# Head products of a small attention layer in half tiles of 64 rows, and the written order of its stage made anew

## The chip, the core and the metric

The kernel runs on one core of a Trainium2 chip. The metric is the device time of one execution in microseconds; the time of a kernel is the median of its runs. A core has five engines that run side by side, each through its own instructions in order: TensorE (matrix products; PE in the profile, its weight loads PEld), VectorE (DVE), ScalarE (ACT), GpSimd (POOL) and SyncE (SP), which here issues nearly all DMAs. Engines wait for each other through semaphores. Products are written to PSUM, which the kernel uses as 8 banks of 128 partitions x 512 numbers; ScalarE and VectorE read them from there.

## The reference, cut to what matters

The program is a small vision tower: patches of 32 images become 256 tokens of 256 features each, then two layers follow, each an attention part and an FFN part. The change lies in the second FFN ("Layer-1 FFN"), which is itself an attention over four heads with four experts each:

```python
sx = jnp.einsum('bsh,ndh->bnsd', x, hl_w) + hl_b[None, :, None, :]      # heads: 4 x 64 rows
q = jnp.einsum('bnsd,neod->bneso', sx, wq)                               # four experts per head
k = jnp.einsum('bnsd,nod->bnso', sx, wk)
v = jnp.einsum('bnsd,nod->bnso', sx, wv)
scores = jnp.einsum('bnesd,bntd->bnest', q, k) * d ** 0.5 + causal
att = jax.nn.softmax(scores, axis=-1)
qkv = jnp.einsum('bnest,bntd->bnesd', att, v)
...
gs = jax.nn.softmax(jnp.einsum('bnsf,nef->bnse', out, gate_w) + gate_b[None, :, None, :], axis=-1)
mixed = jnp.einsum('bnsed,bnse->bnsd', out.reshape(b, nh, s, ne, d), gs)
hn = layernorm(mixed + resid, ln_g, ln_b)
...
hx = jax.nn.relu(jnp.where(pm, 0.0, fx @ fc1_w.T + fc1_b))
hx = jnp.where(pm, 0.0, hx @ fc2_w.T + fc2_b)
hx = layernorm(hx + fx, fnorm_g, fnorm_b)
fg = jax.nn.softmax(fout @ fgate_w.T, axis=-1)
return (fout.reshape(b, s, nh, d) * fg[..., None]).reshape(b, s, h)
```

The line with `sx` is the head product that the change cuts in two: for each image a 256 x 256 weight times the 256 x 256 features. All is 32-bit.

## The kernel before, in words

The stage of the Layer-1 FFN takes the images one by one through about 90 small steps, called pieces. `PIECES` (L1556) is their list; a piece is named by its place there. The steps of one image, in the order of the data, with the engine that does them:

- `features_in` (piece 0, a DMA issued by SP): the normed features come in as `exT`. `heads` (3, L1164, TensorE): the head products, into one bank. `heads_out` (4, ScalarE): into `sx`, with bias; SP issues two DMAs that copy it with the halves of partitions swapped (`sw`).
- `experts` 0, 1 (5, 7, TensorE) and `experts_out` (6, 8, ScalarE, two copies each): the queries `g`. `head_values` (9, TensorE) and `head_values_out` (10, 11, VectorE): `ev`.
- `scores` 0 to 4 (12 to 16, TensorE, two banks each) and `exponentials` (18 to 22, ScalarE): `et`. `outputs` 0 to 3 (31 to 34, TensorE; 0 and 2 take four banks each) and `outputs_out` 0 to 7 (39 to 46, ScalarE).
- `gate_logits`, `gate_softmax`, `mixed`, `summed`, `squares 0`, `squares_sum 0`, `root 0`, `scaled` (47 to 65): VectorE, with `squares`, `root` and one exponential on ScalarE.
- `turn_e` (66): VectorE turns blocks of 32 x 32 and SP writes them to DRAM (`er_turned`). `moved_e` (2, L1435): SP reads them back in another order (`fraw`, two DMAs), which waits until the write has landed. `turned_e` (67, ScalarE): scale and bias into `fxT`. `features_moved` (92): two DMAs of `fxT` to `both`. `features_zero` (68, VectorE) counts zeros.
- `first_layer` (69, TensorE), `first_layer_out` (70, ScalarE, and four DMAs of `hx` to `both`), `second_layer` (71, TensorE), `second_layer_out` (72, 73, VectorE).
- `squares 1` (74), `squares_sum 1` (75), `root 1` (76), `head_gate` 0 to 8 (77 to 85), `last_norm` (86 to 91: 4, 0, 1, 2, 3, and 5, which is the DMA to the output).

What sets the order of the work is written out by hand in two tables. The kernel turns off the scheduler for this stage (`manual_schedule`, L1630), and `order_e` (L1620) yields the pieces: `ROUND` (L1575) is one round, in which each entry is (back, piece), and round r does the piece for image r - back. So -8 is the earliest stage of an image and -1 the last: at one time 8 images are in the pipeline. At the head product of the last image (`LAST`) the rounds stop, and `END` (L1586) lists all that is left, as (how far from the last image, piece). Each engine runs its pieces in the order in which these tables name them. A bank is taken in turn out of 8, so the product that takes a bank waits until the one that had it eight takes ago has been read. Most buffers of the stage exist once or twice (`p1`, `p2`), `et` eight times.

Every product is issued by the helper `mm` at L118, so TensorE's work has one line in the profile, and groups are told apart by their tiles. A product's shape, such as `128*64`, is rows by columns of the array that its weights take. A 32-bit product shows as two records. `halves` is the two slices of 64 partitions.

Of the kernel before, what the change touches and what calls it, by code (L numbers as in the profile page):

```python
# [40 lines left out]
P = 128  # L41
B, N, D = 32, 256, 256
# [38 lines left out]
def vit_tower(tc, a, out):  # L81
# [17 lines left out]
    def bank():  # L99
        return ppool.tile([P, 512], F32, name="bank", tag="bank")  # L100
# [11 lines left out]
    def load(pool, name, eng=nc.scalar):  # L112
        t = pool.tile(list(a[name].shape), F32, name=f"w_{name}")
        eng.dma_start(t, a[name])
        return t

    def mm(o, lhsT, rhs, first=True, last=True):
        nc.tensor.matmul(o, lhsT, rhs, start=first, stop=last)  # L118
# [187 lines left out]
    with (  # L306
# [7 lines left out]
        for k, n in enumerate(PARTS):  # L314
            f = sum(PARTS[:k])
            x, w = pw.tile([P, n, N], F32, name=f"patch0_{k}"), pw.tile([P, n, D], F32, name=f"tokW{k}")
# [4 lines left out]
        p = bank()  # L321
# [296 lines left out]
    hl = load(pwe, "hl_t", nc.sync)  # L618
# [495 lines left out]
    with (  # L1114
# [19 lines left out]
        halves = [slice(h * HD, (h + 1) * HD) for h in range(2)]  # L1134
# [29 lines left out]
        def heads(b, im):  # L1164
            p = im.ph = bank()
            for hp in range(2):
                for k in range(2):
                    mm(p[:, hp * N : (hp + 1) * N], hl[:, k, hp * P : (hp + 1) * P], im.f[:, k], k == 0, k == 1)

        def heads_out(b, im):  # L1170
            im.sx = p2.tile([P, 2, N], F32, name="sx")
# [362 lines left out]
        def last_norm(b, im, i):  # L1534
# [20 lines left out]
        images = [Image() for _ in range(B)]  # L1555
        PIECES = (  # L1556
            (features_in,), (residual,), (moved_e,), (heads,), (heads_out,), (experts, 0), (experts_out, 0),
            (experts, 1), (experts_out, 1), (head_values,), (head_values_out, 0), (head_values_out, 1),
            (scores, 0), (scores, 1), (scores, 2), (scores, 3), (scores, 4), (nothing,), (exponentials, 0),
# [13 lines left out]
            (features_moved,), (count_bad, 0), (count_bad, 1), (count_bad, 2), (count_bad, 3),  # L1573
        )
        ROUND = (  # L1575
            (-2, 2), (-3, 54), (-1, 72), (-3, 56), (-4, 42), (-6, 4), (-1, 73), (-4, 33), (-1, 74), (-4, 34),
            (-4, 44), (-3, 57), (-4, 45), (-1, 75), (-3, 58), (-3, 59), (-6, 1), (-6, 5), (-4, 43), (-1, 76),
            (-4, 46), (-6, 6), (-5, 16), (-5, 12), (-5, 22), (-1, 77), (-6, 30), (-5, 18), (-2, 67), (-6, 9),
            (-1, 87), (-5, 13), (-4, 47), (-5, 14), (-2, 92), (-2, 69), (-6, 10), (-1, 78), (-5, 19),
            (-6, 11), (-1, 79), (-3, 60), (-4, 48), (-5, 20), (-3, 61), (-6, 7), (-5, 15), (-2, 68),  # L1580
            (-1, 80), (-2, 70), (-1, 89), (-3, 62), (-1, 81), (-4, 49), (-1, 82), (-6, 8), (-1, 88),
            (-3, 63), (-3, 64), (-1, 83), (-5, 31), (-1, 84), (-4, 50), (-5, 32), (-1, 85), (-1, 86),
            (-7, 3), (-8, 0), (-1, 90), (-3, 65), (-5, 21), (-4, 51), (-1, 91), (-5, 41), (-3, 66), (-5, 40),
            (-5, 39), (-4, 52), (-4, 53), (-4, 55), (-2, 71), (-1, 93), (-1, 94), (-1, 95), (-1, 96),
        )
        END = (  # L1586
            (0, 2), (3, 51), (4, 65), (2, 40), (3, 52), (2, 39), (2, 42), (2, 41), (2, 21), (0, 1), (3, 53),
            (4, 66), (3, 54), (3, 55), (5, 71), (3, 56), (6, 90), (3, 57), (5, 72), (4, 2), (2, 33), (2, 34),
            (0, 4), (5, 73), (5, 74), (3, 58), (2, 43), (5, 75), (2, 44), (3, 59), (1, 15), (5, 76), (2, 46),
            (2, 45), (5, 77), (2, 47), (5, 78), (6, 91), (2, 48), (0, 7), (1, 21), (4, 67), (3, 60), (0, 9),  # L1590
            (2, 49), (3, 61), (4, 92), (2, 50), (5, 79), (4, 69), (0, 10), (0, 5), (0, 8), (2, 51), (3, 62),
            (2, 52), (5, 80), (0, 11), (5, 87), (2, 53), (3, 63), (1, 13), (4, 70), (3, 64), (2, 54),
            (5, 81), (2, 55), (4, 68), (1, 14), (5, 82), (2, 56), (3, 65), (0, 6), (5, 89), (3, 66), (2, 57),
            (1, 19), (1, 16), (1, 12), (1, 20), (0, 12), (5, 83), (5, 88), (4, 71), (1, 18), (1, 22),
            (2, 58), (0, 18), (4, 72), (3, 2), (4, 73), (2, 59), (4, 74), (4, 75), (1, 31), (1, 32), (1, 33),
            (1, 41), (1, 34), (1, 42), (1, 39), (1, 40), (4, 76), (3, 67), (2, 60), (5, 84), (0, 30),
            (5, 85), (3, 69), (2, 61), (5, 86), (5, 90), (1, 44), (3, 68), (0, 13), (1, 43), (2, 62),
            (1, 45), (2, 63), (3, 92), (1, 46), (5, 91), (3, 70), (0, 14), (1, 47), (4, 77), (0, 16),
            (2, 64), (1, 48), (4, 78), (1, 49), (4, 79), (1, 50), (4, 80), (1, 51), (2, 65), (1, 52),
            (1, 53), (4, 81), (2, 66), (0, 22), (0, 15), (4, 82), (0, 19), (1, 55), (1, 54), (0, 20),  # L1600
            (4, 87), (3, 71), (4, 83), (1, 56), (0, 31), (4, 89), (1, 57), (4, 84), (3, 72), (0, 21),
            (1, 58), (0, 32), (0, 40), (3, 73), (4, 85), (1, 59), (4, 88), (1, 60), (0, 41), (0, 42),
            (3, 74), (2, 2), (3, 75), (0, 39), (2, 67), (1, 61), (0, 33), (0, 43), (4, 86), (4, 90), (0, 34),
            (0, 44), (3, 76), (3, 77), (1, 62), (1, 63), (2, 69), (2, 92), (3, 78), (4, 91), (2, 68),
            (2, 70), (1, 64), (1, 65), (3, 79), (0, 46), (0, 45), (0, 47), (3, 80), (1, 66), (0, 48),
            (3, 81), (0, 49), (3, 87), (3, 82), (1, 2), (2, 71), (0, 50), (3, 83), (0, 51), (3, 89), (0, 52),
            (3, 84), (3, 88), (0, 53), (3, 85), (0, 55), (0, 54), (2, 72), (2, 73), (0, 56), (2, 74),
            (3, 86), (0, 57), (2, 75), (3, 90), (2, 76), (0, 58), (3, 91), (1, 67), (2, 77), (0, 59),
            (2, 78), (0, 60), (2, 87), (2, 79), (1, 92), (0, 61), (2, 80), (2, 89), (1, 69), (2, 81),
            (1, 70), (0, 62), (1, 68), (2, 82), (1, 71), (2, 83), (0, 63), (0, 64), (2, 84), (2, 88),  # L1610
            (2, 85), (0, 65), (0, 66), (2, 90), (1, 73), (0, 67), (1, 72), (2, 86), (0, 69), (0, 92),
            (1, 74), (1, 75), (2, 91), (0, 70), (0, 68), (0, 71), (0, 93), (0, 72), (0, 73), (0, 74),
            (0, 94), (1, 76), (0, 75), (1, 77), (0, 76), (0, 95), (1, 78), (0, 77), (0, 87), (0, 78),
            (1, 79), (1, 87), (1, 80), (0, 79), (0, 96), (1, 81), (0, 80), (1, 82), (1, 89), (1, 83),
            (0, 81), (0, 89), (0, 82), (0, 83), (1, 84), (1, 88), (0, 84), (1, 85), (0, 88), (0, 85),
            (1, 86), (1, 90), (1, 91), (0, 90), (0, 86), (0, 91),
        )
        LAST = PIECES.index((heads,))

        def order_e():  # L1620
# [406 lines left out]
```

## Time and profile before

| | |
|---|---|
| median of 3 runs | 1806.92 us (1803.8 to 1807.66) |
| profiled execution | 1813.98 us, its span 1812.2 us |
| granted TensorE clock | 0.987 |
| TensorE, VectorE, ScalarE busy, of the span | 97%, 72%, 43% |
| first head product of the stage, fifth, last | 1241.0, 1288.2, 1733.6 us |
| all pieces of the stage that are not DMAs done | 1807.6 us |

The profile is of one execution. A row of groups gives line, engine, operation, tiles written and read, shape, count, then busy time in us, mean length of one in ns, idle time before it, and who ended that idle time. A row of waits gives the engine and its instruction, what it waited for, the time in total, how often, and the longest. In the order of time each row has its start, its length, and the group. In the chain that ended last each row has its start, its length and the work that the end hung on. "issue" is time for which the profile shows no reason.

### The profile page before, as it was taken

To read this page: it belongs to the slowest core of one execution; us is meant where nothing else is said; L and a number is where in the kernel's file an instruction comes from. 1 tells how busy PE (TensorE), PEld (TensorE's weight loads), DVE (VectorE), ACT (ScalarE), POOL (GpSimd) and SP (SyncE) were. 2 spreads that over 40 slices of the span, in tenths; PEclk is the share of its full clock that TensorE was granted. 3 is DMA by queue.
4 is the path that set the end of the run, shared out by engine and by line. 5 is a ranking of instruction groups with operands and counts; after the bars stand their busy time and mean duration, and the time that the engine had idled before them with its cause. 6 is when DMAs were issued, how large, how long until landed. Compare 5 with 4: busy or idle time off the path is not lost.

```text
span 1812.2 us, 43832 instructions
## 1 busy us (share of the span) xinstructions
PE 1763.8 (97%) x18072; PEld 1267.4 (70%) x18072; DVE 1309.8 (72%) x3580; ACT 776.5 (43%) x1607; POOL 445.5 (25%) x506
## 2 busy tenths in 40 slices
PE   9999999999999999999999999999999999999993
PEld 7888566667576676767654555557888888888882
DVE  2335367787878665444458877875699999999998
ACT  0000322222222212121244554555888888888883
POOL 1223234343434335333344433341000000000000
PEclk9999999999999999999999999999999999999995
DMA  8552112121211115233312222112244444444432
GB/s 274 180 154 65 35 30 67 51 72 38 59 47 49 57 50 182 91 119 99 112 57 82 75 88 78 74 71 83 68 114 112 115 111 120 109 118 114 122 99 69
DMA packets 197999, 167.93 MB, mean 93 GB/s; under 512 B 71713, under 2 KB 174881, under 8 KB 197409
## 3 DMA queue, kind: packets, MB, share of 16 engines
q1 hardware_dynamic: 191072, 147.49, 28.4%
q0 software_dynamic: 6144, 16.79, 3.1%
q8 instruction: 144, 2.36, 0.6%
q10 hardware_dynamic: 576, 0.79, 0.2%
q14 instruction: 63, 0.51, 0.1%
HBM read 82.95 MB, written 57.41 MB: 77 GB/s over the span
## 4 chain that ended last, share of the span: by engine, by line
PE 85%; DVE 6%; DMA 4%; ACT 4%; issue 1%; SPq 0%; ACTq 0%; DVEq 0%
PE bank L118 85%; DMA er_turned<-eblk 1%; ACT et L1250 1%; DMA fraw<-er_turned 1%; DMA both<-hx 1%; DVE fout L1545 1%; ACT fxT L1449 0%; DMA patch<-in_patches_dram 0%; PE bank L518 0%; DVE eo L1380 0%; ACT g L1206 0%; DVE eblk L1428 0%; DVE ranges L1403 0%; DVE six L126 0%; ACT eo L1285 0%
## 5 line engine op out<-in xcount | busy, mean ns | idle before, releaser
L118 PE MATMUL bank<-ev,et 64*64 64x72 f32 (+3 forms) x6144 | 186.8, 226 | 0.2
L118 PEld LDWEIGHTS bank<-ev,et 64*64 64x64 f32 (+1 forms) x6144 | 171.6, 135 | 10.9 <-ACT hx L1487 1.2
L118 PE MATMUL bank<-tokW,patch 128*128 128x256 f32 x768 | 170.1, 385 | 2.9 <-DMA patch<-in_patches_dram 2.9
L118 PE MATMUL bank<-g,sw 64*64 64x128 f32 (+2 forms) x1280 | 168.0, 377 | 0.0
L1250 ACT ACTIVATE et<-bank 128x512 f32<-128x512 f32 x320 | 167.4, 624 | 1.2 <-PE bank L118 1.2
L118 PE MATMUL bank<-g,sx 64*64 64x128 f32 (+2 forms) x1280 | 167.6, 377 | 0.0
L118 PEld LDWEIGHTS bank<-tokW,patch 128*128 128x128 f32 x768 | 148.5, 194 | 24.9 <-issue 3.8
L118 PE MATMUL bank<-bxT,w_wuv 128*128 128x512 f32 x300 | 131.4, 592 | 0.0
L869 ACT ACTIVATE hT<-bank,cols 128x512 f32<-128x512 f32 x64 | 43.7, 687 | 187.2 <-PE bank L118 122.3
L118 PE MATMUL bank<-wvo,dm 128*128 128x512 f32 x256 | 114.3, 599 | 0.0
L118 PE MATMUL bank<-w_wo,gT 128*128 128x256 f32 x512 | 113.2, 379 | 0.0
L118 PE MATMUL bank<-attn,bv 128*128 128x256 f32 x512 | 113.1, 379 | 0.0
L118 PE MATMUL bank<-w_w,hT 128*128 128x256 f32 x512 | 112.3, 379 | 0.0
L118 PE MATMUL bank<-xsel,w_w 128*128 128x512 f32 x256 | 111.4, 592 | 0.0
L118 PEld LDWEIGHTS bank<-attn,bv 128*128 128x128 f32 x512 | 97.2, 190 | 19.6 <-issue 7.2
L126 DVE BATCH_NORM_STATS2 six<-h 128x6 f32<-128x256 f32 x256 | 105.7, 413 | 4.4
L118 PEld LDWEIGHTS bank<-w_w,hT 128*128 128x128 f32 x512 | 97.0, 190 | 15.6 <-issue 2.9
L118 PEld LDWEIGHTS bank<-w_wo,gT 128*128 128x128 f32 x512 | 97.2, 190 | 13.4 <-DVE gT L491 0.2
L118 PE MATMUL bank<-w_wuv,bxT 128*128 128x512 f32 x240 | 105.4, 592 | 0.0
L1285 ACT COPY eo<-bank 128x280 f32<-128x280 f32 x256 | 89.3, 396 | 36.4 <-PE bank L118 36.4
L118 PEld LDWEIGHTS bank<-bxT,w_wuv 128*128 128x128 f32 x300 | 57.0, 190 | 64.9 <-issue 64.1
L118 PEld LDWEIGHTS bank<-g,sx 64*64 64x64 f32 x1280 | 92.6, 133 | 10.1
(288 smaller groups left out, 3572.3 us busy)
## 6 DMA issues: line engine op xcount, KB each, us to landing
patch<-in_patches_dram SPq DMA_DIRECT2D x31, 768.0 KB
exT<-normed SPq DMA_DIRECT2D x32, 256.0 KB
sw<-sx SPq DMA_DIRECT2D x64, 128.0 KB
er_turned<-eblk SPq DMA_DIRECT2D x31, 256.0 KB
fraw<-er_turned SPq DMA_DIRECT2D x62, 128.0 KB
both<-fxT SPq DMA_DIRECT2D x62, 128.0 KB
both<-hx SPq DMA_DIRECT2D x124, 64.0 KB
out_dram<-fout SPq DMA_DIRECT2D x31, 256.0 KB
```

The source lines that it names most:

```text
L118: nc.tensor.matmul(o, lhsT, rhs, start=first, stop=last)
L126: nc.vector.bn_stats(six, x)
L869: nc.scalar.activation(s.hT[:, m, :], p, AF.Gelu_apprx_tanh, bias=col("b1", m))
L1250: nc.scalar.activation(t2[:, r, :], p, AF.Exp)
L1285: nc.scalar.copy(im.o[:, g * OC : (g + 1) * OC], p[:, 0:OC])
L1545: nc.vector.scalar_tensor_tensor(f[:, g, :], f[:, g, :], im.gate[:, i - 3, n : n + 1], H[b][:, i - 3, d], ALU.mult, ALU.add)
```

## The change

The head product of each image, four products of 128 x 128 weights, becomes eight of 128 x 64; each pair of halves writes the two halves of the partitions of the bank. The table of the round is written anew with 9 stages instead of 8, and the table of the end with 324 entries instead of 305. No other function is changed; `heads` stands in the round between `outputs 0` and `outputs 1` (before: between `outputs 1` and `second_layer`).

```diff
         def heads(b, im):
             p = im.ph = bank()
             for hp in range(2):
                 for k in range(2):
-                    mm(p[:, hp * N : (hp + 1) * N], hl[:, k, hp * P : (hp + 1) * P], im.f[:, k], k == 0, k == 1)
+                    for q in halves:
+                        w = hl[:, k, hp * P + q.start : hp * P + q.stop]
+                        mm(p[q, hp * N : (hp + 1) * N], w, im.f[:, k], k == 0, k == 1)
...
         ROUND = (
-            (-2, 2), (-3, 54), (-1, 72), (-3, 56), (-4, 42), (-6, 4), (-1, 73), (-4, 33), (-1, 74), (-4, 34),
-            (-4, 44), (-3, 57), (-4, 45), (-1, 75), (-3, 58), (-3, 59), (-6, 1), (-6, 5), (-4, 43), (-1, 76),
-            (-4, 46), (-6, 6), (-5, 16), (-5, 12), (-5, 22), (-1, 77), (-6, 30), (-5, 18), (-2, 67), (-6, 9),
-            (-1, 87), (-5, 13), (-4, 47), (-5, 14), (-2, 92), (-2, 69), (-6, 10), (-1, 78), (-5, 19),
-            (-6, 11), (-1, 79), (-3, 60), (-4, 48), (-5, 20), (-3, 61), (-6, 7), (-5, 15), (-2, 68),
-            (-1, 80), (-2, 70), (-1, 89), (-3, 62), (-1, 81), (-4, 49), (-1, 82), (-6, 8), (-1, 88),
-            (-3, 63), (-3, 64), (-1, 83), (-5, 31), (-1, 84), (-4, 50), (-5, 32), (-1, 85), (-1, 86),
-            (-7, 3), (-8, 0), (-1, 90), (-3, 65), (-5, 21), (-4, 51), (-1, 91), (-5, 41), (-3, 66), (-5, 40),
-            (-5, 39), (-4, 52), (-4, 53), (-4, 55), (-2, 71), (-1, 93), (-1, 94), (-1, 95), (-1, 96),
+            (-2, 68), (-5, 47), (-2, 75), (-6, 18), (-7, 9), (-5, 48), (-4, 59), (-1, 78), (-3, 67),
+            (-6, 13), (-5, 49), (-4, 60), (-7, 10), (-6, 19), (-1, 79), (-7, 7), (-3, 92), (-3, 69),
+            (-7, 11), (-7, 8), (-4, 61), (-6, 15), (-5, 50), (-4, 62), (-1, 80), (-1, 87), (-6, 31),
+            (-1, 81), (-1, 89), (-4, 63), (-1, 82), (-3, 70), (-5, 51), (-1, 83), (-4, 64), (-1, 88),
+            (-6, 21), (-8, 3), (-6, 32), (-5, 52), (-6, 39), (-6, 33), (-6, 40), (-4, 65), (-1, 84),
+            (-4, 66), (-6, 41), (-9, 0), (-3, 71), (-6, 42), (-5, 53), (-1, 85), (-1, 90), (-5, 55),
+            (-5, 54), (-1, 86), (-5, 56), (-1, 91), (-6, 34), (-5, 57), (-8, 4), (-6, 43), (-7, 16),
+            (-2, 76), (-4, 2), (-6, 44), (-8, 30), (-3, 72), (-3, 73), (-6, 45), (-6, 46), (-5, 58),
+            (-3, 74), (-8, 1), (-8, 5), (-7, 14), (-7, 22), (-8, 6), (-7, 20), (-2, 77), (-7, 12), (-1, 93),
+            (-1, 94), (-1, 95), (-1, 96),
         )
         END = (
-            (0, 2), (3, 51), (4, 65), (2, 40), (3, 52), (2, 39), (2, 42), (2, 41), (2, 21), (0, 1), (3, 53),
-            (4, 66), (3, 54), (3, 55), (5, 71), (3, 56), (6, 90), (3, 57), (5, 72), (4, 2), (2, 33), (2, 34),
...
+            (3, 52), (0, 2), (4, 65), (5, 68), (2, 39), (4, 66), (3, 53), (6, 76), (2, 32), (6, 77), (3, 54),
+            (0, 4), (3, 55), (4, 2), (6, 78), (2, 42), (2, 40), (7, 84), (2, 41), (2, 33), (2, 44), (3, 56),
...
         )
```

The entries that the new `END` has and the old one had not, because the old rounds had done them by then, are pieces 76 to 89 of the image six back, pieces 84, 85, 86, 90 and 91 of the one seven back, piece 68 of the one five back and piece 32 of the one two back. Pieces 51 (three back) and 21 (two back) are no longer in it.

## The prediction

> **What bounds the kernel now.** I read the engine totals first, then the stretches of the stage that the change touches, then TensorE in order of time, then the waits. The page's first part says that TensorE is the engine to watch, but that is a mean over five stages:
>
> ```profile
> PE 1763.8 (97%) x18072; PEld 1267.4 (70%) x18072; DVE 1309.8 (72%) x3580; ACT 776.5 (43%) x1607; POOL 445.5 (25%) x506
> ```
>
> The Layer-1 FFN starts its first head product at 1241.0 us, the fifth at 1288.2 and the last at 1733.6. The busy times of these stretches (PE, PEld, DVE, ACT, POOL, each with its count) show two regimes:
>
> ```profile
> 1288.20:1733.60 445.40, 441.08 (x11202) 376.48 (x11200) 419.47 (x1249) 374.42 (x941) 0.00 (x0) 1.00 0.43 113
> 1733.60:1770.00 36.40, 33.71 (x892) 28.54 (x888) 36.37 (x107) 28.35 (x72) 0.00 (x0) 1.00 0.38 100
> 1770.00:1808.00 38.00, 12.64 (x124) 7.79 (x124) 34.96 (x128) 12.49 (x35) 0.00 (x0) 0.55 0.26 71
> ```
>
> Up to the last head product TensorE is the bound (99%), with VectorE close behind (94%); from there on VectorE is (36.37 of 36.40 us), up to the last write at about 1808. So work taken from TensorE pays before 1733.6, and work that VectorE still owes at that moment is paid in full after it. 27 rounds take 445.4 us, 16.50 each; the rounds in which nothing is late take 16.26 by the starts of the head products. 445.4 - 27 x 16.26 = 6.4 us are lateness.
>
> TensorE in order of time (start, length, group):
>
> ```profile
> 1482.08 1.04 PE L118 MATMUL bank<-sx,A 64*64 64x256 f32 x16
> ...
> 1486.84 0.23 PE L118 MATMUL bank<-ev,et 128*64 128x72 f32 x2
> 1487.00 1.99 PE L118 MATMUL bank<-exT,w_hl_t 128*128 128x256 f32 x8
> 1488.92 1.17 PE L118 MATMUL bank<-W,both 128*64 128x68 f32 x32
> 1490.02 2.82 PE L118 MATMUL bank<-ev,et 64*64 64x72 f32 x96
> ```
>
> The head product stands between two groups that use the array as two column halves (128*64), and is itself whole (128*128). From the last small product before it to the next group pass 1488.92 - 1486.84 = 2.08 us, for 8 records.
>
> What was late is in the waits (time, times, longest) of 1288 to 1734, and in the chain:
>
> ```profile
> PEld bank L118 <- ACT fxT L1449: 5.2, 6, 1.3
> SPq L1440 <- DMA er_turned<-eblk: 77.5, 27, 4.6
> ...
> 1471.27 4.58 DMA er_turned<-eblk
> 1475.92 0.62 SPq L1440
> 1476.59 2.30 DMA fraw<-er_turned
> 1479.38 1.35 issue
> ```
>
> The turned features go out (er_turned) and come back (fraw), and `turned_e` on ScalarE, then `first_layer` on TensorE, wait when they come late. That is some 5 of the 6.4 us.
>
> **Part 1, the halves.** Four products (8 records) become eight (16 records), each 128 rows by 64 columns by 256 moving elements. The before-trace has no such form; its neighbours are these:
>
> ```profile
> L118 PE MATMUL bank<-exT,w_hl_t 128*128 128x256 f32 x256 | 63.7, 392 | 0.0
> L118 PE MATMUL bank<-W,both 128*64 128x68 f32 x1024 | 42.6, 236 | 9.3 <-DMA both<-hx 8.0 <-ACT both L1481 1.0
> L118 PEld LDWEIGHTS bank<-ev,et 128*64 128x64 f32 x4096 | 129.2, 137 | 5.0
> ```
>
> Rate: the experts' 16 records of 256 elements, four tiles at a time, take 0.87 us from their start to the next group, 0.217 per set; the whole head records start 0.217 apart too. Do two column halves run together? W,both has 32 records in 1490.02 - 1488.92 = 1.10 us, 34 ns each, while 68 elements at 217/256 ns need 58: yes, in pairs. So the new heads are 8 pairs x 0.217 = 1.73 us, and with an entry in the same shape (about 0.06, as between the pairs of one group) 1.79. Before: 2.08, plus 0.05 by which second_layer's first pair is spread after the change of shape. Saved: 0.34 us a round. In ROUND the heads move from between `outputs 1` and `second_layer` to between `outputs 0` and `outputs 1`, all halves; the other changes of shape are as many as before.
>
> Two rules of the Trainium skill bear on this. "TensorEngine Tiling (Array Packing)", Key Properties, says that a change of tiling mode drains the engine; the trace puts the price at 0.10 on entry (0.16 against 0.06) and about 0.2 within and after. Against the change speaks "TensorE: Matmul & The Clock Gate", Part 3, What overlaps: weight loads overlap running products only when their row groups differ. Both halves use all 128 rows, so by the rule each pair would wait for loads, 137 ns at least: 8 x (0.217 + 0.137) = 2.83 us, 0.75 more than now, 24 us over 32 images. The row (34 ns a record with loads of 137 ns) contradicts it; I go by the row. 31 rounds lie ahead of the last head product, where TensorE bounds: **-10.5 us**.
>
> **Part 2, the ROUND.** No instruction is added or removed; the lag grows from 8 rounds to 9.
>
> *Landings.* Before, `turned_e` starts 7.97 us after `turn_e` ends when nothing is late, and 8.4 to 9.5 us when the landing is. After: counted from the start of the heads, `second_layer` ends at 5.6 (heads 1.73, outputs 1 1.07, outputs 2 1.67, itself 1.09 and its end). VectorE's new order from there to `squares_sum 0` is second_layer_out 0.72, mixed 1 1.13, features_zero 0.68, squares_sum 1 0.60, gate_logits 0.68, summed 2.34, head_values_out 0.80, last_norm 1.20, small ones 0.55: 8.7, to 14.3; a wait for ScalarE of 0.6 (below); then squares_sum 0 0.60, last_norm 1 0.68, scaled 0.60, turn_e 0.71, small ones 0.25: 17.75, which is 1.8 after the next heads in a round of 15.95. ScalarE comes to `turned_e` after the end of scores 4 (7.75) and four pieces of 0.95: 11.6. That leaves 9.8 us for the landing, and the late ones fit: **-5 us**. SP's queue: before, `moved_e` waits 77.5 us at its head with the two `sw` issues behind it; after, `sw` goes out ahead of it, and behind it stand only the two issues of `features_moved`, which need `turned_e` anyway. The four `hx` issues (0.67 us each) still have some 4.6 us from `first_layer_out` to `second_layer`, as now (4.7): no change, and the remaining 1.4 us of lateness stay. If that cover is gone, each late landing is a wait of 0.3 to 0.5 us.
>
> *A wait at `outputs 0`.* Its four banks were last used by `scores 1` and `experts 1`, so its fourth product waits for the second copy of `experts_out 1` on ScalarE; behind it stand the rest of the outputs and the heads, and ScalarE's `outputs_out` wait for those. ScalarE from the end of `outputs 3`: two outputs_out 0.56, squares 0.49, four exponentials and experts_out 0 at 0.95 each 4.77, turned_e 0.70, experts_out 1 with its end 1.1, hand-over 0.1: 7.7 us. TensorE between the same points (scores 4, experts 0, scores 2, 0, head values, scores 1, experts 1, first layer, scores 3): 7.5. So 0.2 us of wait. Today the chain ends in `first_layer_out` and costs about as much: outputs 0 takes 1.88 us, its twin outputs 2 1.67. The unknown is how punctual ScalarE is. Ends: -0.1 and +0.6 a round; I take +0.1, near the row: **+3 us** over 27 rounds.
>
> *VectorE.* Its pieces, packed (each length less the 0.083 by which neighbours overlap), sum to 15.04 us an image, 15.2 with the range checks, under the 15.95. `squares_sum 0` will wait about 0.6 to 1.0 us for ScalarE; then 6.65 us of work fit into the 6.55 us up to the end of `second_layer`, and `squares 1` has 0.9 us of slack. It fits, barely.
>
> **Part 3, the END.** It opens at the same head product. More is left for it: of VectorE, for the image six back head_gate 0-4 and 6-8 (0.67 us), last_norm 0, 1, 2 (1.80) and 4 (0.79); for that seven back head_gate 7 and 8 (0.16), last_norm 3 and 4 (1.58); for that five back features_zero (0.68); less a gate_softmax (0.1). Together +5.6 us, in a stretch that VectorE bounds: **+5.5 us**. No other work covers it. On TensorE `outputs 1` of one image moves behind the last head product: **-1 us** ahead of it, hidden after it. VectorE's 5 us of waits near the end (1771, 1795 to 1799) are of the same form and stay.
>
> **Sum.** -10.5 - 5 + 3 + 5.5 - 1 = -8 us. The profiled execution took 1813.98 us: its span 1812.2 becomes about 1804. The median of the runs, 1806.92, is 7 us under the profiled execution; the same 8 us off give **1799 us**.
>
> **Rivals.** *The END costs nothing or the ScalarE wait goes away* (VectorE reaches the last head product ahead of its written place): -8 - 5.5 to -8 - 6, about 1793 and down to 1788. Against it: the first gap on VectorE after 1733.6 is at 1771. 12%.
>
> *VectorE becomes the bound.* If its waits in the round add up to 1.2 us beyond 15.04, rounds stay at 16.26: only the landings are won, -5 + 5.5 - 1: 1806. For it: 94% busy already. 12%.
>
> *Slower, by ScalarE's chain.* If `outputs 0` waits 0.4 us a round more than I took, 11 us over 27 rounds eat the gain; at 0.6 more, 16 us: 1815. It decides from 0.3 on. For it: a chain of nine pieces with one exponential's length of slack anywhere, and `squares 1` of VectorE within it. Against: such a chain stands today and costs 0.2. 17%.
>
> *The halves do not run together*, so the change doesn't do what it says: 16 x 0.217 = 3.5 us, +1.4 us a round, 44 us: 1840 or more. Against: W,both. 3%.
>
> **Numbers.** The likeliest case has 56%, on its own 1793 to 1803. Under 0.2% (3.6 us) this kernel can't be told from unchanged. Faster: 56 + 12 = 68%; same: the VectorE case, 12%; slower: 20%. The range reaches to 1789, into the first rival, and to 1812, into the ScalarE case; the serial case is left out.
>
> **What would show it.** Heads: 16 records of 128*64, 1.8 us to the next group, no gap of 0.3 after them. Rounds: heads 15.9 to 16.1 apart, none at 17.7; the waits of PEld on fxT near zero. `outputs 0`: 1.7 to 2.0 us; over 2.3 is the ScalarE rival. END: from the last head product to the last write 79 to 80 us instead of 74. Wrong it would be if the rounds stay over 16.3, or if a landing of `both` (hx) comes to stand in front of `second_layer`.

## The result and the profile after

The change makes the kernel 3 us faster, where 8 us had been forecast. The median is 1803.62 us (1802.21 to 1807.43, 20 runs) against 1806.64 us (1803.8 to 1809.64, 20 runs) before: a ratio of 0.9984, 95% interval 0.9978 to 0.999. Measured again on another chip it was 1806.11 against 1808.66 us, 0.9979 (0.997 to 0.9988).

The profiled execution took 1804.49 us, its span 1802.7. The engine totals of the changed kernel: 256 more records on TensorE, and as many as before on the other engines.

```profile
PE 1752.5 (97%) x18328; PEld 1245.3 (69%) x18328; DVE 1300.0 (72%) x3580; ACT 774.5 (43%) x1607; POOL 444.3 (25%) x506
```

The stretches of the stage, cut at the first, the fifth and the last head product and at the last write (busy times of PE, PEld, DVE, ACT, POOL; granted clock, DMA share, GB/s):

```profile
1236.80:1282.60 45.80, 45.12 (x1137) 38.07 (x1138) 23.35 (x68) 34.96 (x78) 2.40 (x4) 1.00 0.25 66
1282.60:1719.30 436.70, 434.29 (x11423) 359.82 (x11420) 405.93 (x1224) 372.31 (x940) 0.00 (x0) 1.00 0.44 115
1719.30:1798.40 79.10, 45.98 (x1060) 35.91 (x1055) 77.09 (x261) 42.22 (x111) 0.00 (x0) 0.77 0.32 85
```

The 27 rounds take 436.7 us, where they took 445.4, and are still TensorE's: 434.29 busy of 436.70, at a granted clock of 1.00. The end takes 79.1 us and is VectorE's: 77.09 of 79.10. By the starts of the head products an undisturbed round (15th percentile of their distances) is 16.11 us instead of 16.26, and the lateness (the stretch less 27 of these) 1.9 us instead of 6.4. So two stretches got shorter, by 1.4 and 8.7 us, and the third longer by 5.1.

TensorE in order of time, around one head product (start, length, group):

```profile
1474.23 2.22 PE L118 MATMUL bank<-ev,et 64*64 64x72 f32 x64
1476.28 1.90 PE L118 MATMUL bank<-exT,w_hl_t 128*64 128x256 f32 x16
1478.01 2.91 PE L118 MATMUL bank<-ev,et 128*64 128x72 f32 x96
```

The head product, 16 records now, takes 1478.01 - 1476.28 = 1.73 us to the next group. Ahead of it stands `outputs 0` with 1476.28 - 1474.23 = 2.05 us. The groups of the products in this stage show where TensorE is held (busy, mean ns | idle before, who ended it):

```profile
L118 PE MATMUL bank<-exT,w_hl_t 128*64 128x256 f32 x512 | 60.8, 379 | 0.0
L118 PEld LDWEIGHTS bank<-ev,et 64*64 64x64 f32 x2048 | 43.5, 133 | 11.0 <-ACT g L1208 5.0 <-ACT et L1252 3.5
```

The heads wait for nothing. The products of `outputs 0` do: for the exponentials and for `g`, which is `experts_out` reading the bank that they take over.

The waits between 1288 and 1734 us (time, times, longest), which for this kernel takes in the first 15 us of the end:

```profile
DVE ranges L1405 <- ACT esq L1401: 20.7, 24, 2.2
...
PEld bank L118 <- ACT g L1208: 5.0, 24, 0.3
...
PEld bank L118 <- ACT fxT L1451: 0.2, 1, 0.2
```

TensorE's wait for the landed features is down from 5.2 us to 0.2. In its place stand 24 waits of up to 0.3 us for `experts_out`. VectorE waits most for the squares of ScalarE, 20.7 us.

The chain that ended last, over one and a half rounds of the changed kernel (start, length, work):

```profile
1461.86 9.44 PE bank L118 x269
1471.29 0.66 ACT et L1252
1471.95 0.68 ACT fxT L1451
1472.63 0.53 ACT et L1252 x2
1473.16 0.26 issue
1473.42 0.38 ACT g L1208
...
1473.88 0.70 ACT g L1208
...
1474.63 9.08 PE bank L118 x258
```

Before, landings of DMAs stood in the chain. Now 3.3 us of each such round hang on ScalarE: an exponential, `turned_e` (fxT), two more exponentials, two copies of `experts_out`, and then TensorE goes on, within `outputs 0`.

The other changed kernels are set beside these two in this table; all its stretches are from the one profiled execution of each. "Heads 0 to 4" runs from the first head product to the fifth, "round" is the undisturbed one, "end" runs from the last head product to the last write, and the ratio is to the kernel before on the same chip.

| kernel | median us | ratio (95%) | heads 0 to 4 | 27 rounds | round | lateness | end | stage |
|---|---|---|---|---|---|---|---|---|
| before | 1806.64 | | 47.2 | 445.4 | 16.26 | 6.4 | 73.9 | 566.6 |
| before_again | 1808.91 (one) | | 47.2 | 443.4 | 16.26 | 4.3 | 73.9 | 564.5 |
| after | 1803.62 | 0.9984 (0.9978 to 0.999) | 45.8 | 436.7 | 16.11 | 1.9 | 79.0 | 561.6 |
| after_again | 1806.11 | 0.9979 (0.997 to 0.9988) | 45.8 | 436.3 | 16.10 | 1.4 | 78.5 | 560.6 |
| halves_only | 1804.54 | 0.9989 (0.9979 to 0.9998) | 46.7 | 446.5 | 15.90 | 17.2 | 75.1 | 568.3 |
| order_only | 1812.90 | 1.0029 (1.0018 to 1.0039) | 46.6 | 444.6 | 16.45 | 0.4 | 78.0 | 569.2 |
| after_sq | 1805.12 | 0.9987 (0.9978 to 0.9996) | 45.8 | 435.4 | 16.11 | 0.5 | 79.7 | 560.8 |
| halves_landed | 1798.72 | 0.9937 (0.9918 to 0.9956) | 46.7 | 434.7 | 15.90 | 5.4 | 73.1 | 554.6 |
| after_pool | 1799.48 | 0.9942 (0.9927 to 0.9957) | 45.8 | 430.5 | 15.86 | 2.3 | 79.9 | 556.2 |
| after_noend | 1802.54 | 0.9960 (0.9942 to 0.9979) | 45.8 | 436.6 | 16.11 | 1.7 | 77.4 | 559.8 |
| noend_again | 1802.31 | 0.9966 (0.9952 to 0.9979) | 45.8 | 436.5 | 16.11 | 1.7 | 77.4 | 559.7 |
| halves_pool | 1806.54 | 0.9983 (0.9967 to 0.9999) | 46.7 | 440.7 | 15.66 | 18.0 | 76.4 | 563.8 |

What lies before the first head product is the same program in all, and took 1235.3 to 1241.0 us in these executions; so the stage is compared, and not the span. A profiled execution need not be a typical one: that of `halves_only` was the slowest of its 11 runs (1812.38 us, 7.8 above their median), those of `halves_pool` and `halves_landed` lay 4.9 and 3.7 us above theirs. Their lateness in the table is therefore more than their medians hold.

### The profile page after: what moved, and what is told of

It reads as the page before. It is cut to its first block, busy times and chain, and to the rows that moved or that the text cites. A ratio compares the mean times of both kernels' runs of the same rounds, so it can differ in the third digit from the quotient of the medians.

```text
span 1802.7 us, 44329 instructions
## 1 busy us (share of the span) xinstructions
PE 1752.5 (97%) x18328; PEld 1245.3 (69%) x18328; DVE 1300.0 (72%) x3580; ACT 774.5 (43%) x1607; POOL 444.3 (25%) x506
## 4 chain that ended last, share of the span: by engine, by line
PE 85%; DVE 8%; ACT 4%; issue 1%; DMA 1%; SPq 0%; DVEq 0%; ACTq 0%
PE bank L118 85%; ACT et L1252 2%; ACT g L1208 1%; ACT fxT L1451 1%; DVE fout L1547 1%; DVE eo L1382 1%; DVE ranges L1405 0%; DMA patch<-in_patches_dram 0%; PE bank L518 0%; DVE six L126 0%; DVE two L1390 0%; DVE junk L1186 0%; DVE dx L842 0%; DVE dxB L199 0%; DMA fraw<-er_turned 0%
## 5 line engine op out<-in xcount | busy, mean ns | idle before, releaser
L118 PE MATMUL bank<-ev,et 64*64 64x72 f32 (+3 forms) x6144 | 197.5, 226 | 4.2 <-ACT et L1252 2.4
L118 PEld LDWEIGHTS bank<-ev,et 64*64 64x64 f32 (+1 forms) x6144 | 179.7, 135 | 20.4 <-ACT g L1208 5.0
L118 PE MATMUL bank<-g,sw 64*64 64x128 f32 (+2 forms) x1280 | 178.4, 381 | 0.9 <-issue 0.8
L118 PE MATMUL bank<-g,sx 64*64 64x128 f32 (+2 forms) x1280 | 177.1, 380 | 0.1
L1252 ACT ACTIVATE et<-bank 128x512 f32<-128x512 f32 x320 | 172.8, 628 | 6.1 <-PE bank L118 4.9
```

The source lines that it names most:

```text
L1252: nc.scalar.activation(t2[:, r, :], p, AF.Exp)
```

## The experiments

**The two parts of the change, each alone.** `halves_only` is the old order with the new products:

```diff
-                    mm(p[:, hp * N : (hp + 1) * N], hl[:, k, hp * P : (hp + 1) * P], im.f[:, k], k == 0, k == 1)
+                    for q in halves:
+                        w = hl[:, k, hp * P + q.start : hp * P + q.stop]
+                        mm(p[q, hp * N : (hp + 1) * N], w, im.f[:, k], k == 0, k == 1)
```

> The old ROUND and END with the half products alone. My theory (TensorE bounds the rounds, the halves are worth 0.33 us a round by themselves, the new END costs 5 us): 31 x 0.33 = 10 us less, of which later landings take some 3 back because first_layer comes 0.33 us sooner after turn_e: about 7 us under the kernel before, 1800, and 74 us from the last head product to the last VectorE write. Rival (every gain of TensorE ahead of outputs 0 is eaten by its wait for ScalarE): outputs 0 grows by about 0.2 us and no more than 3 us are won. Rival 2 (VectorE bounds): no change.

The undisturbed round fell from 16.26 to 15.90 us, so the halves are worth 0.36 a round here too. Yet the 27 rounds took 446.5 us in this slow execution, no less than before: 17.2 us are lateness. The median is 2.2 us better, not the 7 expected, and the runs spread from 1802.02 to 1812.38. The waits of this kernel, in the same stretch:

```profile
ACT fxT L1451 <- DMA fraw<-er_turned: 13.6, 12, 2.1
...
PEld bank L118 <- ACT fxT L1451: 12.1, 10, 2.0
```

In the profiled execution TensorE waits 12.1 us behind `turned_e`, and that behind the DMA. The slowest landings take as long as they did (`turned_e` starts up to 9.6 us after `turn_e` ends, 9.5 before); with a shorter round the time that covers them is shorter (7.6 us when nothing is late, 7.97 before), so more of them are late. In the old order the halves pay for this.

`order_only` is the new order with the old products, the same lines the other way round:

```diff
-                    for q in halves:
-                        w = hl[:, k, hp * P + q.start : hp * P + q.stop]
-                        mm(p[q, hp * N : (hp + 1) * N], w, im.f[:, k], k == 0, k == 1)
+                    mm(p[:, hp * N : (hp + 1) * N], hl[:, k, hp * P : (hp + 1) * P], im.f[:, k], k == 0, k == 1)
```

> The new ROUND and END with whole 128-column head products. My theory: the halves are worth 0.33 us a round here too, so this is 10 us slower than the changed kernel: about 1813, 7 us over the kernel before; heads to the next group 1.92 us and outputs 0 still at 2.05. Rival (the wait at outputs 0 eats the gain of the halves): outputs 0 falls back to 1.8 to 1.9 here, and this is at most 4 us slower than the changed kernel: 1807.

Here the landings are covered (lateness 0.4 us), but the undisturbed round is 16.45 us, 0.19 longer than in the old order, and the end costs 4 us more: 1812.90 us, slower than before by 0.29%. TensorE in order of time:

```profile
1481.00 2.22 PE L118 MATMUL bank<-ev,et 64*64 64x72 f32 x64
1483.15 1.99 PE L118 MATMUL bank<-exT,w_hl_t 128*128 128x256 f32 x8
1485.08 2.97 PE L118 MATMUL bank<-ev,et 128*64 128x72 f32 x96
```

The whole heads take 1.93 us to the next group, so the halves save 0.20 of it. The rest lies where the shapes meet: `outputs 0` ahead of the heads goes from 2.15 to 2.05 us and `outputs 1` behind them from 1.12 to 1.07, by the medians of the rounds. The part of `outputs 0` with the wait, its first 32 records, takes 1.03 us with whole heads and with halves, and 0.85 in the old order: the wait belongs to the order. From `order_only` to the changed kernel the median falls by 9.3 us and the round by 0.34. In the traces the order alone loses, the halves alone gain in the round and give it back in the landings, and together the order covers the landings that the halves uncover. The medians do not show that the new order adds anything to the halves: 0.9989 (0.9979 to 0.9998) for the halves alone and 0.9984 (0.9978 to 0.999) for both overlap.

**What the ScalarE chain into `outputs 0` starts from.** `after_sq` takes `squares 1` (74) and its sum out of the place ahead of the exponentials, by less than half a round; `END` gets the same two pieces for the image six back:

```diff
         ROUND = (
...
-            (-5, 47), (-2, 75),
+            (-5, 47),
...
-            (-6, 40), (-4, 65),
+            (-6, 40), (-2, 74), (-4, 65),
...
-            (-5, 56), (-1, 91),
+            (-5, 56), (-2, 75), (-1, 91),
...
-            (-3, 74), (-8, 1),
+            (-8, 1),
```

> The changed kernel with squares 1 (0.6 us of ScalarE) moved from ahead of exponentials 4 to the gap behind outputs_out 1 of the next round, and squares_sum 1 with it. My theory (outputs 0 waits 0.37 us a round because ScalarE comes late through a chain that starts at the end of outputs 3 and has squares 1 in it): outputs 0 falls from 2.05 to about 1.7 us, rounds from 16.11 to 15.8, 9 us over 27 rounds: 1795. Rival (VectorE, with 15.2 us of packed work and its waits, bounds the round at 16.1): rounds stay at 16.1 and the time at 1803. Rival 2 (the wait at outputs 0 is for something else than ScalarE's chain): outputs 0 stays at 2.05.

The round stayed at 16.11 us and `outputs 0` at 2.05: the 9 us expected did not come of taking 0.65 us out from ahead of the chain. ScalarE in order of time shows why:

```profile
1480.67 0.69 ACT L1287 COPY eo<-bank 128x280 f32<-128x280 f32 x2 [0.81 <-PE bank L118]
1481.94 1.08 ACT L1252 ACTIVATE et<-bank 128x512 f32<-128x512 f32 x2 [0.58 <-PE bank L118]
```

Where the squares stood, ScalarE now waits 0.58 us for TensorE (the bracket): the exponentials need `scores 4`. That is where the chain begins, and not at `outputs 3`. In the changed kernel `scores 4` starts at 1466.67 and the first of these exponentials 1.26 us later, and then ScalarE has no gap up to the end of `experts_out 1`, at 1474.58, while TensorE comes to `outputs 0` at 1474.23:

```profile
1467.93 1.09 ACT L1252 ACTIVATE et<-bank 128x512 f32<-128x512 f32 x2
1468.90 1.08 ACT L1208 COPY g<-bank 128x512 f32<-128x512 f32 x2
1469.84 2.11 ACT L1252 ACTIVATE et<-bank 128x512 f32<-128x512 f32 x4
1471.76 0.88 ACT L1451 ACTIVATE fxT<-fraw,cols 128x512 f32<-128x512 f32 x1
1472.46 1.14 ACT L1252 ACTIVATE et<-bank 128x512 f32<-128x512 f32 x2
1473.42 1.16 ACT L1208 COPY g<-bank 128x512 f32<-128x512 f32 x2
```

That is 1.26 + 6.64 = 7.90 us on ScalarE against 1474.23 - 1466.67 = 7.56 on TensorE: a wait of 0.34 us. `outputs 2`, which has no such wait, takes 1.67 us, so by that measure it is 0.38; the old order had 1.88 - 1.67 = 0.21 of it already.

**How far one execution of the kernel before can be trusted.** `before_again` is the kernel before, profiled again.

> The kernel before, unchanged, for a second profile. If the lateness of 6.4 us that I counted in its rounds is what it always has, the 27 rounds again take 445 us and some four of them are over 17 us. If the first profile was an execution with more late landings than most (it was 7 us over the median of the runs), they take 440 to 443.

```profile
1285.60:1729.00 443.40, 440.60 (x11201) 377.32 (x11201) 419.46 (x1249) 374.23 (x941) 0.00 (x0) 1.00 0.43 114
```

The same 27 rounds took 443.4 us here and 445.4 in the first: the undisturbed round is the same to 0.01, the lateness is 4.3 instead of 6.4. So 2 us of what the change could save were an accident of the first profile, which at 1813.98 us was above every one of the 20 runs. `after_again` is the changed kernel once more.

> The changed kernel once more, beside the two below on the same chip. Rounds of 16.11 us with under 2 us of lateness, 79 us from the last head product to the last VectorE write, 3 to 5 us under the kernel before.

Its rounds (16.10), lateness (1.4) and end (78.5) repeat those of the first profile to 0.5 us.

**The chain shortened.** `after_pool` gives `turned_e` to GpSimd, which has nothing to do in these rounds; the rest is the changed kernel:

```diff
-            nc.scalar.activation(..., AF.Identity, bias=col("e_b_t"), scale=col("e_g_t"))
+            nc.gpsimd.tensor_scalar(..., col("e_g_t"), col("e_b_t"), ALU.mult, ALU.add)
```

> The changed kernel with turned_e (0.70 us of ScalarE) done by GpSimd, which has no other work in this stage. My theory, mended after the run that moved squares 1 (outputs 0 waits for ScalarE's seven pieces between the end of scores 4 and the second copy of experts_out 1): the chain is 0.7 us shorter, outputs 0 falls from 2.05 to about 1.7, rounds from 16.11 to 15.8, 9 us less than the changed kernel: 1795. Rival (VectorE bounds the round at 16.1): outputs 0 falls but another wait on TensorE takes its place and the rounds stay at 16.1: 1803. Rival 2 (the wait has nothing to do with ScalarE's load): outputs 0 stays at 2.05: 1803.

The round falls to 15.86 us, `outputs 0` to 1.81 (1.7 was expected), and the median to 1799.48 us, 0.9942 (0.9927 to 0.9957) of the kernel before: faster than both kernels, as this interval lies below that of the changed kernel. The 27 rounds, and the chain in the stretch shown above for the changed kernel:

```profile
1282.80:1713.30 430.50, 429.86 (x11424) 358.36 (x11420) 412.43 (x1224) 358.28 (x913) 26.00 (x27) 1.00 0.44 117
```

```profile
1461.97 24.09 PE bank L118 x600
```

TensorE is busy 429.86 of 430.50 us, and the chain does not leave it. That shows the ScalarE chain to be what held the changed kernel: 0.25 us a round, 6 us over the 27 rounds (436.7 to 430.5).

**The landing taken away.** `halves_landed` is `halves_only` with the features read back from the image before, which have landed long ago; the work is the same:

```diff
-                d = im.d.rearrange("m i q (h x) -> m (q h) i x", h=2)
+                d = images[max(b - 1, 0)].d.rearrange("m i q (h x) -> m (q h) i x", h=2)
```

> The old ROUND and END with the half products, and moved_e reads the turned features of the image before (landed long ago), so that it waits for no landing of er_turned; the numbers that come out are of the wrong image. My theory (the old ROUND's late rounds come from the landing of er_turned and fraw): nearly all rounds fall to 15.9, the 27 rounds from 446 us in the profile of the halves alone to 430, and the time to some 1796. Rival (they come from the landing of hx or from ScalarE's order): the rounds stay spread up to 17.8 and the time at 1804.

Lateness falls from 17.2 to 5.4 us and the median to 1798.72, 0.9937 of before; the undisturbed round is 15.90 as without it. So the landing is what had eaten the gain of the halves in the old order; by the ratios, which do not hang on one execution, it is 9 us. (The edit also takes away the time that `moved_e` stands at the head of SP's queue, 79.7 us in these rounds of `halves_only`; what waited there is named by the waits above, the landing itself.) What is left late is the next transfer, `hx` to `both`:

```profile
PEld bank L118 <- DMA both<-hx: 3.7, 7, 0.7
PE bank L118 <- DMA both<-hx: 2.6, 6, 0.5
```

**Is it ScalarE or the landing that is late in the old order?** `halves_pool` is `halves_only` with `turned_e` on GpSimd, the edit shown above.

> The old ROUND and END with the half products, and turned_e on GpSimd. If the landing of er_turned and fraw itself makes the old order's rounds late, late rounds remain (27 rounds in 436 us or more) and the time is 1800 to 1804. If the rounds were late because turned_e, waiting for its landing, held up the exponentials behind it on ScalarE, they go with it: 27 rounds in 430 us, a tail of 74, and 1793 to 1796, the fastest of all.

The undisturbed round is 15.66 us, so the chain is gone here as well (`outputs 0` 1.66). The lateness stays: 18.0 us, with runs from 1797.2 to 1812.04. The waits of this kernel:

```profile
POOL fxT L1451 <- DMA fraw<-er_turned: 281.1, 16, 46.4
...
PE bank L118 <- POOL fxT L1451: 12.7, 12, 1.9
```

Twelve waits of up to 1.9 us on an engine that had only this piece to do, and whose own idle time ended most often with the landing: ScalarE's load is not the cause of the late rounds, the landing is.

**The end.** `after_noend` is the changed kernel without the `END` entries (6, 76) to (6, 91) and (7, 84), (7, 85), (7, 86), (7, 90), (7, 91), so that two images stay unfinished. They were 5.8 us of VectorE's work by the lengths of the pieces; its busy time in the end fell by 4.6 us:

```diff
         END = (
-            (3, 52), (0, 2), (4, 65), (5, 68), (2, 39), (4, 66), (3, 53), (6, 76), (2, 32), (6, 77), (3, 54),
+            (3, 52), (0, 2), (4, 65), (5, 68), (2, 39), (4, 66), (3, 53), (2, 32), (3, 54),
...
```

> The changed kernel without the pieces that END has for the images six back (root 1, head_gate, last_norm) and seven back (head_gate, last_norm): two images are left unfinished. They are 5.8 us of VectorE in my sum. My theory (VectorE bounds from the last head product on): 79 us from it to the last VectorE write become 73 to 74, and the time falls by 5 to 6 us to about 1798. Rival (the end is set by the chain of the last images through DMAs and TensorE): it falls by less than 2 us, with new idle time on VectorE.

The end became 77.4 us, shorter by 1.6 and not by the 5 to 6 expected. The median of 1802.54 us gives a ratio of 0.9960 (0.9942 to 0.9979), on a chip other than the first one of the changed kernel. So it was run again beside `after_again`.

> The changed kernel without the END's pieces for the images six and seven back (two images are left unfinished), once more, since its profile showed the tail only 1.6 us shorter (77.4) while its times looked 4 us lower on a chip of their own. If the extra 5.8 us of VectorE set the tail by themselves, it is 5 to 6 us under the changed kernel. If TensorE and ScalarE stand close behind VectorE in the END, it is 1 to 2 us under it, and VectorE again waits for outputs and head values in the first 15 us after the last head product.

Again 77.4 us (1.1 less than `after_again`), and in the medians 3.8 less (1802.31 against 1806.11 us), though the intervals of the two ratios overlap (0.9952 to 0.9979, 0.997 to 0.9988). VectorE's share of the end, then VectorE in order of time in this kernel, with its waits in brackets:

```profile
1718.00:1795.40 77.40, 45.62 (x1058) 35.81 (x1054) 72.53 (x232) 41.37 (x108) 0.00 (x0) 0.79 0.30 80
...
1728.06 0.49 DVE L1223 TENSOR_TENSOR ev<-bank,ones_row 128x320 f32<-128x320 f32 x1 [0.75 <-PE bank L118]
...
1731.34 0.69 DVE L1423 TENSOR_TENSOR er<-er,hv 128x512 f32<-128x512 f32 x1 [0.56 <-ACT hv L1413]
...
1739.91 0.36 DVE L1344 RECIPROCAL ranges<-eo 128x16 f32<-128x16 f32 x2 [1.18 <-ACT eo L1287]
...
1741.65 0.92 DVE L1504 TENSOR_TENSOR ey<-bank,c_row 128x272 f32<-128x272 f32 x2 [0.83 <-PE bank L118]
```

These 3.3 us of waits are where the pieces had been. With them gone VectorE arrives early and waits for TensorE and ScalarE. VectorE is busy 72.53 of 77.40 us, against 77.09 of 79.10 with the pieces. So taking the extra work away gives back only a small part of the 5.1 us by which the end grew; why the results that VectorE then waits for come later than before the change, no run shows. The traces put 1.1 to 1.6 us on the pieces, the medians 2 to 4; between these the runs do not decide.

## Why the forecast had the direction and missed the size

Two terms of the sum were mis-sized, both in the direction of too much gain: the wait at `outputs 0` (+3 forecast, +4.6 measured, as its chain was begun at the wrong point) and the landings (-5 forecast, -2.4 to -5.0 by the pairs of profiles). The second tells more in the medians: the forecast took the same 8 us off a median that lay 7 us under the execution from which the -5 was read. By subtraction some 3 of the 5 us that are missing in the medians fall to it; no profile of a run at the median shows them. The halves and `outputs 1` came out as forecast, the end in size only. Step by step:

- **The halves, -10.5 us: right.** 0.34 us a round was forecast; the undisturbed round falls by 0.36 in the old order and by 0.34 to 0.35 in the new (16.45 to 16.11), and from `order_only` to the changed kernel heads 0 to 4 by 0.8 over four rounds: 10.2 us in all. The heads take 1.73 us to the next group, not 1.79. By groups, from `order_only` to the changed kernel, it is 0.20 in the heads, 0.10 ahead of them and 0.05 behind, and the last two are the entry of 0.10 and the spread of 0.05 that the forecast had named. The sentence of the Trainium skill that weight loads overlap only with products of other row groups ("TensorE: Matmul & The Clock Gate", Part 3, What overlaps and what doesn't), taken alone, would have made it 2.83 us, by the estimate of the forecast. The same part also lets a load into the background weight buffer run ahead, which would agree with the 1.73 measured, though no run shows which buffer is used. The row below has 512 loads of 137 ns, between products of which eight pairs pass in 1.73 us, 0.216 a pair, so the loads are hidden although both halves use all rows.

```profile
L118 PEld LDWEIGHTS bank<-exT,w_hl_t x512: 132/137/138, 1236.8 to 1720.6; 128*64 128x64 f32 x171
```

- **The landings, -5 us: the mechanism right, the size taken from too late an execution.** `turned_e` starts 9.93 us after `turn_e` when nothing is late (9.8 forecast), and lateness fell to 1.9. From the first profile that is -4.5, from the second of the kernel before -2.4; with the second profile of the changed kernel (1.4) -5.0 and -2.9. The forecast took all lateness of one execution as the kernel's own, though that execution lay 7 us above the median.
- **The wait at `outputs 0`, +3 us: the place right, the chain begun at the wrong point.** It was priced at 0.1 us a round more than before; it is 0.17 (2.05 against 1.88 us), 4.6 us over 27 rounds; and 2.05 lies over the 1.7 to 2.0 that the forecast gave as its sign. The forecast followed ScalarE from the end of `outputs 3`, with the squares in it, 7.7 us against 7.5. The chain starts when `scores 4` hands over its banks, the squares before it fill a gap (`after_sq`), and it is 7.90 against 7.56. `after_pool`, which takes one piece off it, gives back 0.25 us a round. With the halves this makes the round: 16.26 - 0.35 + 0.17 = 16.08, where 16.11 was measured; the rest is spread over smaller shifts.
- **`outputs 1` moved behind the last head, -1 us: right.** It is also behind the fifth head, so the gain shows once, in heads 0 to 4, and not in the 27 rounds. The products of the outputs on TensorE between the first head and the fifth, before and after (busy, records):

```profile
1241.00:1288.15 47.15, 13.99 (x480) 1.00 0.26 70
```

```profile
1236.84:1282.62 45.78, 13.29 (x448) 1.00 0.25 66
```

One `outputs 1`, 32 records, is missing after. From the second head to the third passed 12.59 us before and 11.55 in `order_only`; with halves 12.45 in the old order and 11.41 in the new: 1.04 us both times.
- **The end, +5.5 us: right in size, in part by luck.** It grew by 5.1, as forecast (79.0 against 79 to 80). But without VectorE's extra pieces it is only 1 to 4 us shorter, and VectorE waits for TensorE and ScalarE where they had been; no experiment took apart what else makes the end longer.

The sum on the first profiles: the forecast had -13.5 us to the last head and +5.5 after it, measured were -10.1 and +5.1, so -5.0 for the stage. The -10.1 are the halves -10.2, `outputs 1` -1.0, the landings -4.5, the wait +4.6, and +1.0 that is left for the rest of the new order, which the forecast had put at nothing. Against the second profile of the kernel before it is -2.9 (561.6 against 564.5) or, with the second profile of the changed kernel, -3.9 (560.6). The medians have -3.0 and -2.6. How late the kernel before usually is rests on two profiles; that they bracket it is likely by the medians, not shown.

Of the rivals, *VectorE becomes the bound* is out: VectorE is busy 405.9 of 436.7 us, and when ScalarE's chain was shortened the round went to 15.86 with the same VectorE work. *Slower, by ScalarE's chain* named the right mechanism, at 0.07 us a round above the 0.1 that was taken; it would have decided from 0.3 on. *The END costs nothing or the ScalarE wait goes away* is out: the end grew by 5.1 us, and the wait by 0.17 a round. *The halves do not run together* is out by the row of the heads.

## What to carry to other kernels

A faster piece on the bound engine shortens the cover of every transfer that is timed by the round; look for the landing that has least slack before counting the gain, and see that the order moves with it. A chain through a second engine is measured from the hand-over that starts it (the last product that it waits for) and not from the piece ahead of it, since work ahead may only fill a gap. And a saving of lateness needs more than one profile of the kernel before: the undisturbed round was the same to 0.01 us in two executions, the lateness 6.4 and 4.3.

## What was not expected of the hardware

How far the runs of a kernel spread went with how much they hang on the landing: 10.4 us (1802.0 to 1812.4) with halves in the old order and 14.8 (1797.2 to 1812.0) with `turned_e` on GpSimd in it, 11 runs each, against 4.8 for the changed kernel in 11 runs, 2.7 for `order_only` in 8 and 3.2 for `after_pool` in 6. GpSimd's add and multiply on 128 x 512 numbers takes about 0.97 us, and while it runs an addition on VectorE mostly takes longer. (In `after_pool` 14 of the 18 additions of `summed 1` that overlap with it by over 0.3 us take 0.97 to 1.09 us, the other 4 and the 7 beside them 0.68 to 0.69.) The group of `summed 1` from 1300 to 1700 us, first in the changed kernel:

```profile
L1393 DVE TENSOR_TENSOR er<-two 128x512 f32<-128x512 f32 x25 | 17.0, 679 | 0.0
```

and in `after_pool`:

```profile
L1393 DVE TENSOR_TENSOR er<-two 128x512 f32<-128x512 f32 x25 | 21.5, 859 | 0.0
```

VectorE was busy for 412.43 of the 430.50 us there, and the round still got shorter, so no cost of these 0.18 us an image is seen.
